# Step sizes of a selective-scan layer: projected on four column groups of the array and expanded in a series by another engine

## The chip, the core and the metric

The kernel runs on one core of a Trainium2 chip. The metric is the device time of one execution in microseconds, taken as the median of several runs. In what follows PE is the matrix engine (PEld its weight loads), DVE the vector engine, ACT the scalar engine, POOL the GpSimd engine and SP the engine that issues most transfers; SBUF is the on-chip memory, PSUM the memory that PE writes to, in banks of 128 x 512 floats.

## What is computed

The input is 4 sequences of 1,024 tokens with 256 features, in float32. A mixer layer comes first, then a mixture of experts; each is added to its input and normalised. What matters here is how the mixer gets its step sizes:

```python
zxbcdt = u @ in_proj_w.T                       # 512 z, 768 xBC, 8 dt columns
A  = -jnp.exp(A_log).mean(axis=0)              # 8 heads
z, xBC, dt = jnp.split(zxbcdt, [512, 1280], axis=-1)
xBC = silu(causal_conv_of_4(xBC) + conv_b)
x, Bm, Cm = jnp.split(xBC, [512, 640], axis=-1)
dt = softplus(dt + dt_bias)                    # one step per token and head
dA = exp(dt * A)
h  = h * dA + x * (dt * Bm)                    # for each token in turn
y  = h @ Cm + D * x
y  = rmsnorm(y) * silu(z);  x1 = layernorm(u + y @ out_proj_w.T)
```

After that x1 goes through a shared expert and through the two of eight experts that a softmax router chooses, and through a second layer normalisation.

## The kernel before, in words

The 4,096 tokens are worked in 8 tiles of 512 and 32 chunks of 128 (four chunks to a tile). For each tile, `turn_u` transposes the input into `uT`, `channels` projects and convolves the six groups of 128 xBC channels, and `steps` makes the step sizes of the tile, 128 tokens x 32 numbers (four chunks, eight heads). For each chunk the recurrence is worked as matrix products: `decays` loads running decays from DRAM and scans them on DVE, `turn_x` transposes x, B and C, `within` and `across` form the output and pass the state `h` on, `mix_out` gates and projects, `deviations` normalises, `turn_x1` transposes the result and `shared` runs the shared expert. `route` and `scatter` choose experts and scatter the rows to DRAM by indirect transfers that POOL issues. After the chunks, 71 blocks of 128 rows go through their experts (`chosen`), and `finish` normalises and writes out.

`steps` is a chain of six pieces. `project` (L435) multiplies the tokens, as 128 x 128 weights, with 8 columns of the projection matrix `win`, for four chunks and two halves of the features: 8 matmuls in source, 16 passes in the trace, since each float32 matmul is two. `begin` (L448) adds the bias on DVE and forms w = -|x|. `exponential` (L460) takes exp(w) on ACT. `series`, `series_on` and `step` (L463 to L489) work softplus on DVE as max(x, 0) + 2 atanh(w / (w + 2)), with a polynomial of five coefficients in q = s*s, and end with `dt` and `a` = dt * A. `step_decays` (L494) then sums `a` along the tokens on PE (a transpose, L502, and three products, L504), takes exponentials on ACT, and sends the decays to DRAM, from where `decays` loads them.

The order of work is written out by hand: `put(place, f)` gives each piece a place in time, the pieces are sorted by place and issued in that order, so that every engine has a fixed queue. A chunk has a slot of 16.4 places. The steps of tile n+2 stand in the fourth slot of tile n (L1514), those of tiles 0 and 1 at the start (L1488, L1503); `step_decays` of a tile stands in the first slot of the tile before it. PSUM has three banks `ps_m` for chunk work, two `ps_h` for expert products, two `ps_p` for projections (with `uT` transposes and the steps), one `ps_z`.

The piece `one` of `turn_x1` (L867) writes a row of ones over row 0 of the transposed x1, by POOL, once a chunk; the shared expert's first products then carry the biases in that row.

The loads of `win` are cut in pieces (L166 to L172): on SP its last 8 columns, then xBC columns 256 to 511, then 512 to 767, then z; on ACT xBC columns 0 to 255.

Of the kernel before, what the change touches and what calls it, by code (L numbers as in the profile page):

```python
# [8 lines left out]
F32 = mybir.dt.float32  # L9
# [3 lines left out]
ALU = mybir.AluOpType  # L13
# [15 lines left out]
D_PROJ = D_INNER + CONV_DIM + N_HEADS  # L29
# [4 lines left out]
NSUB = T // P  # L34
# [13 lines left out]
SERIES = (0.33333334, 0.19999853, 0.14296179, 0.10853288, 0.11612165)  # L48
# [9 lines left out]
R_DTB = 0  # L58
R_ALOG = R_DTB + N_HEADS
# [6 lines left out]
def kernel(  # L66
# [17 lines left out]
    nc = tc.nc  # L84
# [25 lines left out]
    ps_p = pool_in(ctx, "ps_p", 2, space=PSUM)  # L110
# [12 lines left out]
    def bc(ap, shape):  # L123
        return ap.to_broadcast(shape)
# [7 lines left out]
    def put(place, f, *args):  # L132
        pieces.append((place, len(pieces), f, args))
# [23 lines left out]
    win = const.tile([P, KD, D_PROJ], F32, name="win")  # L157
    rows_sb = const.tile([P, R_ALL], F32, name="rows_sb")
# [54 lines left out]
    a_neg = const.tile([P, N_HEADS], F32, name="a_neg")  # L213
# [182 lines left out]
    def by_head(t):  # L396
        return t.rearrange("p (c h) -> p c h", h=N_HEADS)

    def head_row(ap):
        return bc(ap.unsqueeze(1), [P, NSUB, N_HEADS])  # L400

    def bank(pool, tag, name):
        return pool.tile([P, T], F32, tag=tag, name=name)
# [21 lines left out]
        put(s + places[1], out_of, 0)  # L425
        put(s + places[2], out_of, 1)

    def steps(at, s, places=(0.0, 1.9, 3.2, 6.8, 10.8, 13.0), ps=(ps_p, "pp")):

        st = tile_state[at]  # L430

        def small(tag, n=NS):
            return k2.tile([P, n], F32, tag=tag, name=f"{tag}_{at}")

        def project():  # L435
            uT = st["uT"]
            pd = st["pd"] = bank(*ps, f"pd_{at}")
            for c in range(NSUB):
                for k in range(KD):
                    nc.tensor.matmul(  # L440
                        pd[:, c * N_HEADS : (c + 1) * N_HEADS],
                        uT[:, k, c * P : (c + 1) * P],
                        win[:, k, D_PROJ - N_HEADS :],
                        start=(k == 0),
                        stop=(k == KD - 1),
                    )

        def begin():  # L448
            x = st["dt_x"] = small("dt_x")
            nc.vector.tensor_tensor(  # L450
                by_head(x), by_head(st["pd"][:, :NS]), head_row(rows_sb[:, R_DTB:R_ALOG]),
                ALU.add,
            )

            w = st["dt_w"] = small("dt_w")
            nc.vector.scalar_tensor_tensor(w, x, -1.0, x, ALU.mult, ALU.min)

        def exponential():  # L460
            nc.scalar.activation(st["dt_w"], st["dt_w"], AF.Exp)

        def series():  # L463
            w = st["dt_w"]
            s = small("dt_s")
            nc.vector.tensor_scalar_add(s, w, 2.0)
            nc.vector.reciprocal(s, s)
            nc.vector.tensor_mul(s, s, w)
            q = small("dt_q")
            nc.vector.tensor_mul(q, s, s)  # L470
            acc = small("dt_acc")
            nc.vector.tensor_scalar_mul(acc, q, SERIES[4])
            st.update(dt_s=s, dt_q=q, dt_acc=acc)

        def series_on():
            q, acc = st["dt_q"], st["dt_acc"]
            for x in SERIES[3:0:-1]:
                nc.vector.scalar_tensor_tensor(acc, acc, x, q, ALU.add, ALU.mult)

        def step():  # L480
            q, acc, s, x = st["dt_q"], st["dt_acc"], st["dt_s"], st["dt_x"]
            nc.vector.scalar_tensor_tensor(acc, acc, SERIES[0], q, ALU.add, ALU.mult)
            nc.vector.scalar_tensor_tensor(acc, acc, 1.0, s, ALU.add, ALU.mult)
            nc.vector.tensor_scalar_max(x, x, 0.0)
            dt = small("dt")
            nc.vector.scalar_tensor_tensor(dt, acc, 2.0, x, ALU.mult, ALU.add)
            a = small("a")
            nc.vector.tensor_tensor(by_head(a), by_head(dt), head_row(a_neg), ALU.mult)
            st.update(dt=dt, a=a)  # L489

        for place, f in zip(places, (project, begin, exponential, series, series_on, step)):
            put(s + place, f)

    def step_decays(at, s, places=(0.0, 3.3, 7.5), ps=(ps_p, "pp")):  # L494
# [358 lines left out]
    def turn_x1(k):  # L853
        ch = chunk_state[k]

        def turn():
            pt = ch["ptx"] = bank(ps_m, "ps", f"ptx_{k}")
            for j in range(KD):
                nc.tensor.transpose(
                    pt[:, j * P : (j + 1) * P], ch["x1"][:, j * P : (j + 1) * P], ident  # L860
                )

        def copy():
            x1T = ch["x1T"] = k3.tile([P, KD, P], F32, tag="x1T", name=f"x1T_{k}")
            nc.scalar.copy(x1T.rearrange("p k t -> p (k t)"), ch["ptx"][:, :D])

        def one():  # L867
            nc.gpsimd.memset(ch["x1T"][0:1, 0], 1.0)

        return {"ptx": turn, "x1T": copy, "one": one}  # L870

# [596 lines left out]
    for k in range(NCHUNK + 1):  # L1468
        ps = deviations(k)
# [15 lines left out]
    H2 = (ps_h, "ph")  # L1485
    turn_u(0, -25.0)
    channels(0, 0, -20.9, -11.0)
    steps(0, -19.2, (0.0, 1.9, 2.4, 2.7, 2.7, 2.7), H2)  # L1488
    for c, s in zip(range(1, NCC), (-17.4, -15.7, -14.0, -10.0, -8.3)):
        channels(0, c, s, max(s + 5.0, -10.9), H2 if c in (2, 4) else (ps_p, "pp"))  # L1490
    step_decays(0, -12.4, (0.0, 0.9, 6.0), H2)
# [8 lines left out]
    load_shared(2.0)  # L1500
    for j in range(3):
        put((2 + j) * SLOT, clear_sum, j)
    steps(1, -0.3, (0.0, 8.0, 9.0, 15.5, 18.5, 21.5))  # L1503
    n_first = 0
    for k in range(NCHUNK):
        at, i = divmod(k, NSUB)
        s = k * SLOT
# [120 lines left out]
```

## Time and profile before

| | |
|---|---|
| median of 3 runs | 881.39 us (879.44 to 884.99) |
| profiled execution: its own time | 876.08 us |
| its span, first to last instruction | 874.1 us |
| around the span | 2.0 us |
| granted PE clock, mean | 0.983 |
| PE busy | 821.5 us (94%) |
| DVE busy | 588.2 us (67%) |
| ACT busy | 449.8 us (51%) |
| POOL busy | 425.2 us (49%) |

The busy shares are means over two stages: the chunks, up to about 575 us, and the blocks that overlap with their end and run on to the end. Times on a line of the timeline are the start from the beginning of the span, then how long the instructions of that line took together, engine, source line, operation, tiles, count, and in brackets how long the engine had been idle before and what released it.

### The profile page before, as it was taken

Reading aid. Unit: us, or ns where it says so; the run is one execution under the profiler, and the core shown is the slowest. Engines: PE = TensorE matmul, PEld = TensorE weight load, DVE = VectorE, ACT = ScalarE, POOL = GpSimd, SP = SyncE. Lnnn points to the kernel's source line nnn. Section 1 sums busy time; section 2 is a strip of 40 time slices with the busy share of each in tenths; the row PEclk is TensorE's granted clock in tenths of the full one; section 3 lists DMA queues with packets and bytes.
Section 4 is the critical chain, followed back from the end, with each engine's and each line's share of the span. In section 5 each row is a group of like instructions: output and inputs, shape, how many; then the busy total and the mean of one; then the engine's idle time right before and its main releaser. Section 6 shows DMA issues by size and latency. Waiting matters only on the chain.

```text
span 874.1 us, 13379 instructions
## 1 busy us (share of the span) xinstructions
PE 821.5 (94%) x3795; PEld 574.0 (66%) x3795; DVE 588.2 (67%) x1549; ACT 449.8 (51%) x1069; POOL 425.2 (49%) x563
## 2 busy tenths in 40 slices
PE   7789999999999999999998999899999999999980
PEld 4556677766767767666655776677677777776660
DVE  5897878878878879798788666245833333366653
ACT  4465657556657466676464455354444444444430
POOL 3253434457556556456724843624733333365443
PEclk9899999999999999999999999999999999999996
DMA  5547263174274363343321631335644432467764
GB/s 152 164 96 252 59 158 91 38 166 91 82 170 93 99 143 90 112 122 93 106 76 44 188 73 25 86 74 117 147 63 66 62 56 31 85 165 169 170 158 113
DMA packets 89381, 94.92 MB, mean 109 GB/s; under 512 B 15831, under 2 KB 78813, under 8 KB 89309
## 3 DMA queue, kind: packets, MB, share of 16 engines
q1 hardware_dynamic: 68030, 67.08, 26.3%
q0 software_dynamic: 18464, 24.33, 17.9%
q10 hardware_dynamic: 2816, 2.67, 1.0%
q8 instruction: 32, 0.52, 0.3%
q14 instruction: 39, 0.32, 0.1%
HBM read 61.22 MB, written 32.83 MB: 108 GB/s over the span
## 4 chain that ended last, share of the span: by engine, by line
PE 55%; issue 13%; DVE 11%; POOL 10%; DMA 7%; ACT 3%; POOLq 0%; SPq 0%; DVEq 0%; ACTq 0%
PE ph_s L883 6%; PE pp L554 6%; PE ph_c L883 6%; PE py L730 6%; POOL acc L1363 6%; PE pmo L815 5%; PE pz L632 5%; PE po_s L917 5%; DMA acc<-yb_c,to_c 4%; DVE xbc L572 3%; DMA fin<-acc 3%; PE po_c L917 3%; PE pi L751 2%; PE pst L767 2%; POOL xs L1102 2%
## 5 line engine op out<-in xcount | busy, mean ns | idle before, releaser
L883 PE MATMUL ph_c<-w,xgT_c 128*128 x568 | 193.0, 463 | 4.9 <-DVE xgT_c L1336 3.6
L1363 POOL DMA_INDIRECT acc<-yb_c,to_c x71 | 114.6, 1614 | 156.8 <-ACT yb_c L1357 95.5
L883 PEld LDWEIGHTS ph_c<-w,xgT_c 128*128 128x128 f32 x568 | 97.1, 190 | 47.9 <-DVE xgT_c L1336 5.6
L895 DVE TENSOR_TENSOR hid<-h_c,ph_c 128x352 f32<-128x352 f32 x71 | 36.9, 519 | 126.1 <-PE ph_c L883 118.5
L572 DVE SCALAR_TENSOR_TENSOR xbc<-pp,cols_sb,xbc 128x509 f32<-128x509 f32 x144 | 107.1, 745 | 16.3 <-ACT tail L580 8.9
L917 PE MATMUL po_c<-w,hT_c 128*128 x426 | 104.3, 381 | 1.2 <-ACT hT_c L912 1.2
L901 ACT ACTIVATE hid<-hid 128x352 f32<-128x352 f32 x103 | 51.8, 502 | 87.9 <-DVE hid L895 81.2
L554 PE MATMUL pp<-uT,win 128*128 128x512 f32 x192 | 92.0, 605 | 0.6 <-ACT dec L511 0.5
L883 PE MATMUL ph_s<-sw,x1T 128*128 128x352 f32 (+1 forms) x256 | 82.9, 465 | 2.1 <-issue 1.4
L763 POOL TENSOR_TENSOR y<-y,yi 128x512 f32<-128x512 f32 x28 | 35.5, 1267 | 99.5 <-ACT yi L757 79.7
L1102 POOL DMA_INDIRECT xs<-x,r_idx x64 | 73.4, 1147 | 20.5 <-issue 11.5
L917 PEld LDWEIGHTS po_c<-w,hT_c 128*128 128x128 f32 x426 | 75.5, 190 | 9.5 <-ACT hT_c L912 1.7
L657 DVE TENSOR_TENSOR_SCAN el<-da,ident 128x512 f32<-128x512 f32 x64 | 78.4, 1227 | 0.0
L883 PEld LDWEIGHTS ph_s<-sw,x1T 128*128 128x128 f32 x256 | 48.0, 191 | 35.1 <-issue 13.2
L890 ACT COPY h_c<-ph_c 128x352 f32<-128x352 f32 x71 | 32.1, 453 | 62.8 <-PE ph_c L883 54.4
L730 PEld LDWEIGHTS py<-xdt,el 128*128 128x128 f32 x512 | 62.4, 193 | 1.4
L815 PE MATMUL pmo<-wout,yT 128*128 128x256 f32 x256 | 61.4, 383 | 0.3 <-ACT yT L810 0.2
L730 PE MATMUL py<-xdt,el 128*128 128x64 f32 x512 | 61.3, 273 | 0.0
L632 PE MATMUL pz<-win,uT 128*128 128x512 f32 x128 | 61.2, 601 | 0.0
L587 ACT ACTIVATE xbc<-xbc 128x512 f32<-128x512 f32 x48 | 30.1, 629 | 58.7 <-DVE xbc L582 39.0
L757 ACT ACTIVATE yi<-pi,dec 128x64 f32<-128x64 f32 x224 | 49.0, 330 | 13.2 <-PE pi L751 10.6
L563 ACT ACTIVATE xbc<-pp,cols_sb 128x512 f32<-128x512 f32 x48 | 37.3, 779 | 34.9 <-PE pp L554 32.4
(214 smaller groups left out, 1548.4 us busy)
## 6 DMA issues: line engine op xcount, KB each, us to landing
da<-dad SPq DMA_DIRECT2D x64, 256.0 KB
xg_c<-xs SPq DMA_DIRECT2D x71, 130.0 KB
fin<-acc SPq DMA_DIRECT2D x32, 256.0 KB
w<-in_w_dram SPq DMA_DIRECT2D x16, 352.0 KB
w<-neg_d POOLq DMA_DIRECT2D x16, 352.0 KB
acc<-pad SPq DMA_DIRECT2D x3, 1408.0 KB
x<-in_u_dram SPq DMA_DIRECT2D x32, 128.0 KB
acc<-acc SPq DMA_DIRECT2D x32, 128.0 KB
```

Of the source, the lines that this page charges most:

```text
L554: nc.tensor.matmul(pp, win[:, k, D_INNER + c * P : D_INNER + (c + 1) * P], st["uT"][:, k], start=(k == 0), stop=(k == KD - 1),)
L572: nc.vector.scalar_tensor_tensor(cv[:, o:], hold["pp"][:, : T - o], cols_sb[:, cw + j : cw + j + 1], cv[:, o:], ALU.mult, ALU.add,)
L632: nc.tensor.matmul(pz, st["uT"][:, j, tok], win[:, j, :D_INNER], start=(j == 0), stop=(j == KD - 1),)
L657: nc.vector.tensor_tensor_scan(el, ch[f"da{j}"], ident4.rearrange("p h t -> p (h t)"), 0.0, ALU.mult, ALU.add)
L730: nc.tensor.matmul(py[:, hd], m, ch["xdt"][:, hd], start=True, stop=True)
L757: nc.scalar.activation(yi[:, hd], ch["pi"][:, hd], AF.Copy, scale=st["dec"][:, h0 + h : h0 + h + 1],)
L815: nc.tensor.matmul(po[:, :D], ch["yT"][:, c * P : (c + 1) * P], wout[:, c], start=(c == 0), stop=(c == NYC - 1),)
L883: nc.tensor.matmul(pw[:, : rhs.shape[-1]], hold["xT"][:, k], rhs, start=(k == 0), stop=(k == KD - 1),)
L901: nc.scalar.activation(t[:, :H], t[:, :H], AF.Silu)
L917: nc.tensor.matmul(po[:, :D], hold["hT"][:, c * P : (c + 1) * P], weights(None, c), start=(c == 0), stop=(c == HCK - 1),)
L1102: s = nc.gpsimd.indirect_dma_start(out=xs, out_offset=bass.IndirectOffsetOnAxis(ap=idx[:, j : j + 1], axis=0), in_=x1, in_offset=None, bou ...
L1363: s = nc.gpsimd.indirect_dma_start(out=accd[b % 2], out_offset=bass.IndirectOffsetOnAxis(ap=hold["to"], axis=0), in_=hold["yb"], in_offset ...
```

## The change

The eight matmuls of `project` swap their operands. The projection columns become the weights (the last 32 columns of `win`: 24 xBC columns and the 8 of dt) and the tokens stream through, 128 at a time; the four chunks go to four groups of 32 array columns and so to four groups of 32 partitions of a PSUM bank, chunk by chunk within each half of the features. Two pieces are added behind it: `copy`, in which ACT copies the 128 x 128 result to SBUF, and `turn`, a transpose on PE into a second bank. `begin` reads the 8 useful columns of each 32. In the series DVE keeps w + 2 (now halved, so that the factor 2 at the end goes away) and the reciprocal; the rest is 14 small POOL instructions, with the polynomial in two halves, in place of 11 DVE instructions. The places of the pieces change with it. `one` becomes a copy of a row of ones by ACT.

```diff
-    def steps(at, s, places=(0.0, 1.9, 3.2, 6.8, 10.8, 13.0), ps=(ps_p, "pp")):
+    def steps(at, s, places=(0.0, 0.6, 1.6, 2.0, 3.2, 6.8, 10.8, 13.0), ps=(ps_p, "pp")):
...
         def project():
             uT = st["uT"]
-            pd = st["pd"] = bank(*ps, f"pd_{at}")
-            for c in range(NSUB):
-                for k in range(KD):
+            pd = st["pdT"] = bank(*ps, f"pdT_{at}")
+            for k in range(KD):
+                for c in range(NSUB):
                     nc.tensor.matmul(
-                        pd[:, c * N_HEADS : (c + 1) * N_HEADS],
+                        pd[32 * c : 32 * c + 32, :P],
+                        win[:, k, D_PROJ - 32 :],
                         uT[:, k, c * P : (c + 1) * P],
-                        win[:, k, D_PROJ - N_HEADS :],
                         start=(k == 0),
                         stop=(k == KD - 1),
+                        tile_position=(0, 32 * c),
                     )
+        def copy():
+            st["dtT"] = k1.tile([P, P], F32, tag="dtT", name=f"dtT_{at}")
+            nc.scalar.copy(st["dtT"], st["pdT"][:, :P])
+        def turn():
+            pd = st["pd"] = bank(*ps, f"pd_{at}")
+            nc.tensor.transpose(pd[:, :P], st["dtT"], ident)
...
         def series():
             w = st["dt_w"]
-            s = small("dt_s")
-            nc.vector.tensor_scalar_add(s, w, 2.0)
+            s, q, q2, lo, hi = (small(f"dt_{n}") for n in ("s", "q", "q2", "lo", "hi"))
+            nc.vector.tensor_scalar(s, w, 2.0, 0.5, ALU.add, ALU.mult)
             nc.vector.reciprocal(s, s)
-            nc.vector.tensor_mul(s, s, w)
-            q = small("dt_q")
-            nc.vector.tensor_mul(q, s, s)
-            acc = small("dt_acc")
-            nc.vector.tensor_scalar_mul(acc, q, SERIES[4])
+            pool.tensor_tensor(s, s, w, ALU.mult)
+            pool.tensor_tensor(q, s, s, ALU.mult)
+            pool.tensor_tensor(q2, q, q, ALU.mult)
+            pool.tensor_scalar(hi, q, c4, c3, ALU.mult, ALU.add)
         def series_on():
-            for x in SERIES[3:0:-1]:
-                nc.vector.scalar_tensor_tensor(acc, acc, x, q, ALU.add, ALU.mult)
+            pool.tensor_scalar(lo, q, c2, c1, ALU.mult, ALU.add)
+            pool.tensor_tensor(hi, hi, q2, ALU.mult)
+            pool.tensor_tensor(hi, hi, lo, ALU.add)
+            pool.tensor_tensor(hi, hi, q2, ALU.mult)
+            pool.tensor_scalar(lo, q, c0, 1.0, ALU.mult, ALU.add)
         def step():
-            nc.vector.scalar_tensor_tensor(acc, acc, SERIES[0], q, ALU.add, ALU.mult)
-            nc.vector.scalar_tensor_tensor(acc, acc, 1.0, s, ALU.add, ALU.mult)
-            nc.vector.tensor_scalar_max(x, x, 0.0)
-            nc.vector.scalar_tensor_tensor(dt, acc, 2.0, x, ALU.mult, ALU.add)
-            nc.vector.tensor_tensor(by_head(a), by_head(dt), head_row(a_neg), ALU.mult)
+            pool.tensor_tensor(hi, hi, lo, ALU.add)
+            pool.tensor_tensor(hi, hi, s, ALU.mult)
+            pool.tensor_scalar(x, x, 0.0, None, ALU.max)
+            pool.tensor_tensor(dt, hi, x, ALU.add)
+            pool.tensor_tensor(by_head(a), by_head(dt), head_row(a_neg), ALU.mult)
...
         def one():
-            nc.gpsimd.memset(ch["x1T"][0:1, 0], 1.0)
+            nc.scalar.copy(ch["x1T"][0:1, 0], ones[0:1])
...
-    steps(0, -19.2, (0.0, 1.9, 2.4, 2.7, 2.7, 2.7), H2)
+    steps(0, -19.2, (0.0, 0.5, 0.9, 1.3, 1.8, 2.3, 2.3, 2.3), H2)
...
-    steps(1, -0.3, (0.0, 8.0, 9.0, 15.5, 18.5, 21.5))
+    steps(1, -0.3, (0.0, 4.0, 6.0, 8.0, 9.0, 14.5, 17.5, 20.5))
```

More of the change, by code (lines that the diff above doesn't have):

```diff
@@ L450, in begin @@
             nc.vector.tensor_tensor(
-                by_head(x), by_head(st["pd"][:, :NS]), head_row(rows_sb[:, R_DTB:R_ALOG]),
+                by_head(x), st["pd"][:, :P].rearrange("p (c h) -> p c h", c=NSUB)[:, :, 32 - N_HEADS :], head_row(rows_sb[:, R_DTB:R_ALOG]),
                 ALU.add,
@@ L461, in exponential @@
             nc.scalar.activation(st["dt_w"], st["dt_w"], AF.Exp)
+        c0, c1, c2, c3, c4 = (x * 0.25 ** (i + 1) for i, x in enumerate(SERIES))
+        pool = nc.gpsimd
         def series():
             w = st["dt_w"]
-            s = small("dt_s")
-            nc.vector.tensor_scalar_add(s, w, 2.0)
+            s, q, q2, lo, hi = (small(f"dt_{n}") for n in ("s", "q", "q2", "lo", "hi"))
+            nc.vector.tensor_scalar(s, w, 2.0, 0.5, ALU.add, ALU.mult)
             nc.vector.reciprocal(s, s)
-            nc.vector.tensor_mul(s, s, w)
@@ L469, in series @@
-            q = small("dt_q")
-            nc.vector.tensor_mul(q, s, s)
-            acc = small("dt_acc")
-            nc.vector.tensor_scalar_mul(acc, q, SERIES[4])
-            st.update(dt_s=s, dt_q=q, dt_acc=acc)
-        def series_on():
-            q, acc = st["dt_q"], st["dt_acc"]
-            for x in SERIES[3:0:-1]:
-                nc.vector.scalar_tensor_tensor(acc, acc, x, q, ALU.add, ALU.mult)
+            pool.tensor_tensor(s, s, w, ALU.mult)
+            pool.tensor_tensor(q, s, s, ALU.mult)
@@ new lines, in series @@
+            pool.tensor_tensor(q2, q, q, ALU.mult)
+            pool.tensor_scalar(hi, q, c4, c3, ALU.mult, ALU.add)
+            st.update(dt_s=s, dt_q=q, dt_q2=q2, dt_lo=lo, dt_hi=hi)
+        def series_on():
+            q, q2, lo, hi = (st[f"dt_{n}"] for n in ("q", "q2", "lo", "hi"))
+            pool.tensor_scalar(lo, q, c2, c1, ALU.mult, ALU.add)
[3 more added lines that the diff above has]
+            pool.tensor_scalar(lo, q, c0, 1.0, ALU.mult, ALU.add)
@@ L480, in step @@
         def step():
-            q, acc, s, x = st["dt_q"], st["dt_acc"], st["dt_s"], st["dt_x"]
-            nc.vector.scalar_tensor_tensor(acc, acc, SERIES[0], q, ALU.add, ALU.mult)
-            nc.vector.scalar_tensor_tensor(acc, acc, 1.0, s, ALU.add, ALU.mult)
-            nc.vector.tensor_scalar_max(x, x, 0.0)
+            lo, hi, s, x = (st[f"dt_{n}"] for n in ("lo", "hi", "s", "x"))
+            pool.tensor_tensor(hi, hi, lo, ALU.add)
+            pool.tensor_tensor(hi, hi, s, ALU.mult)
@@ L485, in step @@
+            pool.tensor_scalar(x, x, 0.0, None, ALU.max)
             dt = small("dt")
-            nc.vector.scalar_tensor_tensor(dt, acc, 2.0, x, ALU.mult, ALU.add)
+            pool.tensor_tensor(dt, hi, x, ALU.add)
             a = small("a")
-            nc.vector.tensor_tensor(by_head(a), by_head(dt), head_row(a_neg), ALU.mult)
+            pool.tensor_tensor(by_head(a), by_head(dt), head_row(a_neg), ALU.mult)
             st.update(dt=dt, a=a)
-        for place, f in zip(places, (project, begin, exponential, series, series_on, step)):
+        for place, f in zip(
+            places, (project, copy, turn, begin, exponential, series, series_on, step)
+        ):
```

## The prediction

> **What bounds the kernel now.** I read the sums by stage first, then the costs of the groups, then the order of PE around the steps, and last the places where PE waits. The first view gives busy time by stretches of 62.8 us, about four chunks (PE, PEld, DVE, ACT, POOL, then the granted clock):
>
> ```profile
> 83.80:146.60 62.80, 61.98 (x295) 42.92 (x295) 47.81 (x92) 39.98 (x99) 25.21 (x34) 1.00 0.45 114
> 335.00:397.80 62.80, 61.80 (x292) 42.48 (x292) 54.41 (x129) 40.42 (x104) 34.61 (x50) 1.00 0.42 108
> 397.80:460.60 62.80, 58.30 (x281) 40.60 (x281) 50.46 (x107) 35.62 (x81) 34.89 (x52) 0.97 0.35 96
> ```
>
> From 84 to 398 us PE is busy for 98 to 99%, so there a microsecond off PE is a microsecond off the time, and relief of DVE is worth nothing by itself. Before 84 us (55.0 of 62.8 us busy) and after 398 us PE waits for others. The groups that are touched, and the rows that price what is new:
>
> ```profile
> L440 PEld LDWEIGHTS pd<-win,uT 128*128 128x128 f32 x128 | 15.6, 192 | 4.0 <-issue 3.1 <-ACT uT L422 0.7 <-DMA neg<-in_w_dram 0.2
> L440 PE MATMUL pd<-win,uT 128*128 128x8 f32 x128 | 14.8, 251 | 0.0
> L689 ACT COPY b<-pb 128x128 f32<-128x128 f32 x32 | 8.2, 255 | 1.8 <-PE pb L682 1.8
> L502 PEld LDWEIGHTS pc<-ident,a 128*32 128x32 f32 x8 | 0.8, 96 | 4.6 <-DVE xbc L572 3.0 <-issue 1.0 <-ACT xbc L587 0.5
> ```
>
> The first two overlap, so what a tile pays is read from starts in the timeline:
>
> ```profile
> 83.00 1.85 PE L440 MATMUL pd<-win,uT 128*128 128x8 f32 x16
> 84.70 2.64 PE L883 MATMUL ph_s<-sw,x1T 128*128 128x352 f32 x8
> ...
> 103.43 1.88 PE L554 MATMUL pp<-uT,win 128*128 128x512 f32 x4
> 105.15 0.27 PE L502 MATMUL pc<-ident,a 128*32 128x128 f32 x1
> 105.15 0.30 PEld L504 LDWEIGHTS pc<-a,le 128*128 128x128 f32 x2 [0.33 <-issue]
> 105.26 0.31 PE L504 MATMUL pc<-a,le 128*128 128x32 f32 x2
> ```
>
> The old projection holds PE from 83.00 to 84.70: 1.70 us for 16 passes, 0.106 each, the spacing of 128-column weight loads. L502 is the one instruction that already uses 32 columns (128*32): its 128 streamed columns occupy PE for 0.11 us, and it starts when the product before it has streamed (103.43 + 4 x 0.43 = 105.15).
>
> POOL's price for small dependent instructions, its free time in a steps slot, and the one place where POOL sets the pace (the last four lines, from the chain of waits):
>
> ```profile
> 421.34 0.21 POOL L531 TENSOR_TENSOR part<-tail,cols_sb 128x12 f32<-128x12 f32 x1
> 421.63 0.21 POOL L536 TENSOR_TENSOR corr<-corr,part 128x12 f32<-128x12 f32 x1
> 421.92 0.21 POOL L531 TENSOR_TENSOR part<-tail,cols_sb 128x6 f32<-128x6 f32 x1
> ...
> 224.52 0.20 POOL L868 MEMSET x1T<- 1x128 f32 x1 [3.02 <-ACT x1T L865]
> 228.95 1.26 POOL L763 TENSOR_TENSOR y<-y,yi 128x512 f32<-128x512 f32 x1 [4.23 <-ACT yi L757]
> ```
>
> ```profile
> 430.41 0.28 POOL shift L843
> 430.72 0.60 ACT x L847
> 433.02 0.37 ACT hT_s L912
> 433.44 1.56 PE po_s L917 x6
> ```
>
> **The projection.** Removed: 1.70 us of PE a tile. Added: 16 passes of 128 streamed columns. If the four groups run fully side by side, 4 x 0.107 = 0.43 us; if a weight load of 0.096 stands ahead of every pass, 16 x (0.096 + 0.107) = 3.25 us. L502's load did not stand alone: PE shows no gap ahead of 105.15, and L504's loads run under L502's own product. So loads stay hidden. The two passes of one float32 matmul go to the same 32 columns, so I let them follow each other, and let only the next chunk's pass overlap. That makes pairs: 8 x 0.107 = 0.86 us. The transpose adds 0.11 (L502's spacing). Gain: 1.70 - 0.86 - 0.11 = 0.73 us a tile, between 1.16 and -1.66. [...]
>
> **The added wait.** `turn` on PE waits for ACT's copy, 0.255 us by L689. From tile 2 on the first shared-expert product (1.2 us) stands between them on PE, and ACT has finished `yi` at 84.09 when the projection ends at about 83.9: the copy is done by 84.4, the transpose due at 85.1. Without that cover it would cost about 0.5 us. For tile 1 the cover is missing (below). The second bank is no wait: both buffers that it could take were emptied by the `uT` copies that the projection itself needs.
>
> **DVE's relief.** 11 instructions a tile, 2.27 us by their means (0.19 each, 0.30 and 0.27 the longest). From 84 to 398 us PE covers DVE, so 0.
>
> **POOL's load.** 14 instructions a tile. Dependent ones stand 0.29 apart (421.34, 421.63, 421.92), nine of the gaps are dependent; independent ones 0.13 to 0.20 (r_info, 406.02, 406.15, 406.28): 9 x 0.29 + 5 x 0.2 = 3.6, taken as 3.8 us. The longest such rows (1.05 and 1.20 us) bound it at some 15 us, the shortest (0.13) at 1.8. They stand behind xw in POOL's queue, in tiles 4 to 7 partly ahead of the scatters. What covers them is POOL's idle time before y_yi or fade: 9.2 us in tile 2, 8.5 in tile 3, 7.3 in tile 4 (the two lines), 6.5 and 7.2 in tiles 5 and 6. So 0 there. In tile 7 POOL has no gap from 409.9 to 430.7: six scatter transfers, corr, four more, fade, roots, then ACT's normalisation waits for shift, hT_s stands behind that on ACT, and PE's po_s behind hT_s. There the 3.8 us go straight into the chain, less 0.2 for the memset: +3.6, less PE's 0.73: +2.9.
>
> **The ones.** 32 POOL memsets of 0.20 become ACT copies of 0.15 to 0.26 (L580, L689): 5 to 8 us of ACT, whose next work after x1T waits over 1 us for PE (97.40 to 98.75), while the shared product starts at 100.27. Cost 0. The only PE wait for a memset (0.9 us, before 422.60) lies ahead of the hT_s wait of tile 7, which takes it over: 0.
>
> **The start.** Tile 0's projection now also needs the load of xBC columns 512 to 767. Loads issued up to it are 1,356 KB; the transfer rates of the first 40 us add up to 1,389 KB at 7 us, and the projection starts at 9.1: no stall, at most 8.7 us (pp_4 reads them at 17.84 without a wait). POOL brings `a` about 1.2 us later than DVE did (15.93), PE's pc and pp_4 move by as much, and ACT's four silu then end near 22.6 instead of 23.3: a gain of up to 0.6. SP's decay store goes 1.2 us later; the decays had landed by 23 and are read at 28.55. Tile 1: ACT's copy stands behind silu of its first group, which waits for DVE:
>
> ```profile
> 39.87 0.63 ACT L587 ACTIVATE xbc<-xbc 128x512 f32<-128x512 f32 x1 [6.04 <-DVE xbc L582]
> ```
>
> The copy ends at 40.8 instead of leaving PE free to begin pb at 38.74, so pb, px and the next projection go 2.2 us later, of which 0.6 was idle anyway; DVE and ACT lose about 1.1. Then DVE, busy without a break from 43 to 57, drops 2.8 us of instructions (48.92 to 55.18). POOL's y_yi goes from 53.18 to about 55.3, which takes back 1 us. POOL's third weight correction is put behind four series pieces, about 3 us later, and is read at 68. Together -1.0, between -3.1 (all relief, no wait) and +2.2 (the wait, no relief).
>
> **Sum.** -1.0 for the start, 5 x -0.73 = -3.65 for tiles 2 to 6, +2.9 for tile 7: -1.75, so 876.08 becomes 874.3. The profiled execution lies 5.3 us below the median of the runs; on the median's scale 881.39 becomes **879.6 us**.
>
> **Rivals.**
> - Other side: POOL becomes late in every slot. DVE and POOL lengthen each other: corr took 1.05 us at 420.32, DVE's dt_w averages 0.75 with 0.19 at best. Against it, medians of 0.21 to 0.24. It decides from 0.5 us an instruction (7 us against gaps of 6.5 to 9.2). At 0.65 (9.1 us) tiles 3 to 6 lose 0.6, 1.8, 2.6 and 1.9, tile 7 8.2: -4.65 + 6.9 + 8.2 = +10.4, 891.8; at 0.75 about +19.
> - The groups don't overlap at all, loads hidden: 1.71 us, 0.12 lost a tile: -1.0 + 0.6 + 3.7 = +3.3, 884.7. With loads exposed: +8.3 (tiles 2 to 6) + 5.3 - 1.0 = +12.6, 894.0.
> - Faster: four groups side by side (5 x 1.16), all 3.1 us at the start, and tile 7's lateness given back later by idle PE: -8.9, 872.5.
>
> **How the numbers follow.** Forecast 0.60; no overlap 0.12; loads exposed 0.06; POOL late 0.12; all gains 0.10. A measurement of this kernel tells about 1% (8.8 us) from no change. Faster by over 1% is the last case, 0.10; within 1% the first two, 0.72; slower the loads and POOL, 0.18. Range 870 to 893: from the fast case, less the runs' scatter, to POOL at 0.65 us, leaving out exposed loads and POOL's worst.
>
> **What would show it.** Right: from the projection's first start to the next product 0.8 to 1.0 us, the transpose 0.11 without a wait from tile 2 on, y_yi still released by ACT's yi, a PE wait of about 4 us for hT_s near 433, pb of chunk 1 near 41. Wrong: a spacing of 0.2 per pass, POOL instructions over 0.5, y_yi released by series pieces, or a tile 0 projection that waits for its load.

## The result and the profile after

The changed kernel takes 882.59 us (median of 20 runs, 878.63 to 888.32), the kernel before, beside it on the same chip, 879.38 us (20 runs, 876.59 to 884.99). The ratio is 1.0032, 95% interval 1.0019 to 1.0045: slower by 0.3%, where 0.2% faster was forecast. The time lies in the forecast range. In the profiled executions the spans are 882.0 and 874.1 us.

To find the place, I compare when PE starts the four transposes `pt` of the gated product, once a chunk. A shift is that start less the start in the profile before. These sums of shifts by stage are worked out from the timelines, for the changed kernel and for the kernels of the experiments below ("in slots" are the four stretches between chunks 6-7, 10-11, 14-15 and 18-19, in which the steps of tiles 3 to 6 are projected; us, negative is earlier than before):

| kernel | start, to chunk 2 | tile 2 (2-3) | tiles 3-6, in slots | rest of 3-22 | tile 7's projection (22-23) | 23 to 25 | 25 to 31 |
|---|---|---|---|---|---|---|---|
| changed | -0.01 | -0.90 | +0.33 | -0.13 | -0.93 | **+7.64** | -0.27 |
| series on DVE | +0.76 | -0.90 | +0.36 | -0.13 | -0.94 | -0.71 | -0.23 |
| before, series on POOL | -3.38 | 0.01 | +0.13 | +4.26 | -0.01 | +6.02 | -0.40 |
| tile 7's series on DVE | -0.45 | -0.90 | +0.37 | -0.12 | -0.94 | +0.70 | -0.18 |
| projection only | +0.71 | -0.90 | +0.31 | -0.13 | -1.02 | -0.69 | -0.06 |
| norm behind hT_s | -1.92 | -0.90 | +0.35 | -0.14 | -0.93 | +0.77 | -0.07 |
| PE kept busy | -1.55 | -0.91 | +0.35 | -0.12 | -0.94 | +5.47 | -0.68 |
| begin late | -3.48 | -0.90 | -1.37 | +7.07 | +0.03 | +8.36 | -0.04 |
| copy early | -3.55 | -0.90 | +0.32 | -0.15 | -0.93 | +6.90 | -0.24 |
| second choice late | -2.81 | -0.90 | -3.14 | -0.21 | -0.51 | +6.90 | +2.25 |
| before, second choice late | +3.08 | 0.00 | -0.05 | +1.84 | +0.43 | 0.00 | +3.05 |
| ones by POOL | -1.43 | -0.90 | +0.32 | +2.40 | -1.02 | +6.40 | -0.27 |
| before, norm behind hT_s | +2.24 | 0.01 | +0.12 | -0.04 | -0.01 | -1.69 | -0.59 |
| all moves | -3.29 | -0.90 | -3.15 | -0.22 | -0.43 | -2.90 | +2.07 |
| all, second choice in the early tiles | -2.85 | -0.90 | -3.16 | -0.18 | -0.93 | -2.86 | -0.88 |
| the same, copy late | -3.68 | -0.90 | -3.15 | -0.18 | -0.93 | -2.86 | -0.11 |
| the same, tile 7's series on POOL | -3.67 | -0.90 | -3.16 | -0.18 | -0.93 | +0.73 | +0.88 |

Line numbers in what follows are those of each kernel itself. The middle columns repeat within 0.1 us from profile to profile, where the queues are the same. Two parts do not: the start (0 to +3.1 for three kernels whose start is that of before), and what the blocks add behind chunk 31 (-2.7 to +3.3 in all profiles, +2.2 in this one, in a stage that the change leaves alone). So a single pair of spans says little, and a stage of the table much.

The lines that answer to the old projection's 1.70 us. After, on PE, tile 2:

```profile
83.08 0.64 PE L442 MATMUL pdT<-uT,win 128*32 128x128 f32 x16
83.66 1.45 PE L902 MATMUL ph_s<-sw,x1T 128*128 128x352 f32 x4
84.94 0.27 PE L457 MATMUL pd<-ident,dtT 128*128 128x128 f32 x1
85.05 1.38 PE L902 MATMUL ph_s<-sw,x1T 128*128 128x360 f32 x4
```

The 16 passes hold PE from 83.08 to 83.66, 0.58 us, and the transpose for 0.11 us without a wait: 1.0 us less a tile, better than forecast. The table shows 0.90 and 0.93 of it kept in tiles 2 and 7, and nothing in tiles 3 to 6. Tile 4's slot, PE and then DVE (the bracket is the idle time ahead, and what ended it):

```profile
206.75 0.39 PE L878 MATMUL ptx<-ident,x 128*128 128x128 f32 x2
...
209.66 0.64 PE L442 MATMUL pdT<-uT,win 128*32 128x128 f32 x16
...
213.18 0.60 PE L704 MATMUL px<-ident,xbc 128*128 128x128 f32 x4
215.53 0.63 PE L823 MATMUL pt<-ident,xw 128*128 128x128 f32 x4 [1.75 <-DVE xw L805]
```

```profile
207.03 0.69 DVE L752 TENSOR_TENSOR y<-y,py 128x512 f32<-128x512 f32 x1 [0.60 <-PE py L749]
...
211.84 0.19 DVE L461 TENSOR_TENSOR dt_x<-pd,rows_sb 128x32 f32<-128x32 f32 x1 [0.53 <-PE pd L457]
212.06 0.99 DVE L469 SCALAR_TENSOR_TENSOR dt_w<-dt_x 128x32 f32<-128x32 f32 x1
...
214.71 0.68 DVE L805 TENSOR_TENSOR xw<-y,pz 128x512 f32<-128x512 f32 x1
```

From the end of PE's `py` DVE needs 8.4 us to the end of `xw` (207.03 to 215.39; before 8.2), idle only for the 0.53 us in which `dt_x` waits for the turn. PE's own work in that stretch is now 7.0 us, so it waits 1.75 us (before 0.68). Whatever PE saves there is returned as a longer wait. The same place in the profile before:

```profile
215.06 0.52 DVE L895 TENSOR_TENSOR hid<-h_s,ph_s 128x352 f32<-128x352 f32 x1 [0.23 <-ACT xdt L779]
215.58 0.68 DVE L786 TENSOR_TENSOR xw<-y,pz 128x512 f32<-128x512 f32 x1
216.40 0.63 PE L804 MATMUL pt<-ident,xw 128*128 128x128 f32 x4 [0.68 <-ACT x L692]
```

DVE's only slack on this way was the 0.23 us that it stood idle ahead of `hid` (tile 6 the same, tiles 3 and 5 none). The bracket of `pt` names ACT's copy x, but `pt` starts 0.15 us after the end of `xw` in each of these slots, before and after. Tile 7's place before (POOL, then PE) and after (PE, ACT and POOL):

```profile
409.65 0.26 POOL L843 TENSOR_SCALAR shift<-stat 128x1 f32<-128x1 f32 x1
...
430.41 0.27 POOL L843 TENSOR_SCALAR shift<-stat 128x1 f32<-128x1 f32 x1
...
433.44 1.56 PE L917 MATMUL po_s<-sw_sb,hT_s 128*128 128x256 f32 x6 [0.75 <-ACT hT_s L912]
434.84 1.89 PE L730 MATMUL py<-xdt,el 128*128 128x64 f32 x16
```

```profile
425.46 0.28 PE L521 MATMUL pc<-ident,a 128*32 128x128 f32 x1 [2.06 <-POOL a L505]
...
437.23 2.93 PE L936 MATMUL po_s<-sw_sb,hT_s 128*128 128x256 f32 x6 [6.30 <-ACT hT_s L931]
439.95 2.78 PE L749 MATMUL py<-xdt,el 128*128 128x64 f32 x16
```

```profile
434.51 0.60 ACT L866 ACTIVATE x<-x,shift,stat 128x256 f32<-128x256 f32 x1 [6.48 <-POOL shift L862]
435.13 1.28 ACT L527 ACT_TABLE_LOAD   x1
...
436.72 0.46 ACT L931 COPY hT_s<-pt_s 128x384 f32<-128x384 f32 x1
```

```profile
407.90 0.26 POOL L862 TENSOR_SCALAR shift<-stat 128x1 f32<-128x1 f32 x1
...
410.13 1.16 POOL L483 TENSOR_TENSOR dt_s<-dt_s,dt_w 128x32 f32<-128x32 f32 x1
...
421.24 0.21 POOL L491 TENSOR_SCALAR dt_lo<-dt_q 128x32 f32<-128x32 f32 x1
...
425.16 0.25 POOL L505 TENSOR_TENSOR a<-dt,a_neg 128x32 f32<-128x32 f32 x1
...
432.20 1.10 POOL L383 TENSOR_SCALAR stat<-stat 128x2 f32<-128x2 f32 x1
...
434.21 0.27 POOL L862 TENSOR_SCALAR shift<-stat 128x1 f32<-128x1 f32 x1
```

POOL has no gap from 408 to 437, but for some 0.3 us ahead of each scatter transfer. The three pieces of the series hold it from 410.13 to 412.25, 421.24 to 422.67 and 423.89 to 425.35, 5.0 us together; `shift` ends up 5.55 us later behind the previous chunk's `shift` than before (26.31 us against 20.76). ACT's normalisation waits for it, `hT_s` stands behind that on ACT, PE's `po_s` behind `hT_s`. PE waits 6.30 us (before 0.75: 5.55 us more), and then `po_s` and `py` take 2.93 and 2.78 us where 1.56 and 1.89 were seen before: another 2.2 us. The granted clock is 0.50 in the first of the two.

### The profile page after: what moved, and what is told of

It is laid out like the page before. It is cut to its first block, busy times and chain, and to the rows that moved or that the text cites. A ratio compares the mean times of both kernels' runs of the same rounds, so it can differ in the third digit from the quotient of the medians.

```text
span 882.0 us, 13404 instructions
## 1 busy us (share of the span) xinstructions
PE 818.9 (93%) x3803; PEld 564.8 (64%) x3803; DVE 570.7 (65%) x1461; ACT 458.7 (52%) x1109; POOL 453.6 (51%) x643
## 4 chain that ended last, share of the span: by engine, by line
PE 53%; issue 14%; POOL 10%; DVE 10%; DMA 9%; ACT 3%; SPq 1%; POOLq 0%; DVEq 0%; ACTq 0%
PE pp L573 7%; PE ph_s L902 6%; PE py L749 6%; POOL acc L1382 6%; PE pmo L834 6%; PE pz L651 5%; DMA acc<-yb_c,to_c 5%; PE po_s L936 5%; PE ph_c L902 5%; DMA fin<-acc 3%; PE pi L770 2%; DVE xbc L591 2%; PE po_c L936 2%; PE pst L786 2%; POOL xs L1121 2%
## 5 line engine op out<-in xcount | busy, mean ns | idle before, releaser
L573 PE MATMUL pp<-uT,win 128*128 128x512 f32 x192 | 95.4, 624 | 1.7 <-ACT uT L422 1.2
L936 PE MATMUL po_s<-sw_sb,hT_s 128*128 128x256 f32 x192 | 48.3, 389 | 7.2 <-ACT hT_s L931 7.2
```

The costliest lines, as they stand in the source:

```text
L573: nc.tensor.matmul(pp, win[:, k, D_INNER + c * P : D_INNER + (c + 1) * P], st["uT"][:, k], start=(k == 0), stop=(k == KD - 1),)
L936: nc.tensor.matmul(po[:, :D], hold["hT"][:, c * P : (c + 1) * P], weights(None, c), start=(c == 0), stop=(c == HCK - 1),)
```

## The experiments

Each is an edit of the changed kernel unless it says "before". Ratios are to the kernel before, with 95% intervals.

### Which part costs: the series, and where

**Series on DVE.** All of the series as in the kernel before, the rest as changed.

```diff
-            pool.tensor_tensor(s, s, w, ALU.mult)
...
+            nc.vector.tensor_mul(s, s, w)
...
```

> The changed kernel with the whole series back on DVE (the 11 instructions of before); the projection on four column groups, its copy and turn, and the ones by ACT stay. Theory (POOL's queue at tile 7 makes the loss): the 7.8 us that the changed kernel loses between chunks 24 and 25 are gone, PE's wait for hT_s near 433 is under 1.5 us and po_s takes about 1.6 us again; but the start keeps its wait for the copy without DVE's relief behind it, so the gated transposes of chunk 2 start 1.5 to 3 us later than before, and tiles 3 to 6 keep nothing of the cheaper projection. End of the span -1 to +2 us against before, ratio 0.998 to 1.003. Rival (the projection's own steps cost the time: the wait of DVE for the turn, the transposes, the copies on ACT): the transposes of chunk 25 still start at 449 or later, ratio 1.004 or more.

874.75 us, ratio 0.9948 (0.9925 to 0.997), better than either theory had it. Chunks 23 to 25 cost 0.7 us less than before instead of 7.6 more. PE still waited 2.73 us for `hT_s` there, not under 1.5 as expected, but `po_s` took 1.56 us; chunk 2 came 0.76 us later than before, not 1.5 to 3. The projection, its copy and turn are not what costs.

**Before, series on POOL.**

```diff
-            nc.vector.tensor_mul(s, s, w)
...
+            pool.tensor_tensor(s, s, w, ALU.mult)
...
```

> The kernel before with the series on POOL alone; projection, ones by POOL and all places of before. Theory: DVE's relief at the start makes chunk 2 about 1 us earlier, nothing is gained or lost in tiles 3 to 6, and between chunks 24 and 25 the queue of POOL costs 6 to 8 us as in the changed kernel, with an idle stretch of PE of over 5 us near 431 to 437 and po_s slowed to some 2.9 us behind it. End of the span +4 to +8 us, ratio 1.003 to 1.009. Rival (the projection's steps cost it): no loss at tile 7, ratio 1.000 or less.

884.9 us, 1.006 (1.0037 to 1.0084). The loss at tile 7 is there (+6.0), in another form: the memset stands behind the series in POOL's queue. The same cost a stretch that I had not expected, 3.6 us between chunks 15 and 16 (PE, then POOL):

```profile
289.69 4.35 PE L888 MATMUL ph_s<-sw,x1T 128*128 128x352 f32 x8 [2.05 <-POOL x1T L873]
```

```profile
289.25 0.25 POOL L493 TENSOR_TENSOR a<-dt,a_neg 128x32 f32<-128x32 f32 x1
289.45 0.19 POOL L873 MEMSET x1T<- 1x128 f32 x1
```

At the start, with DVE's relief alone, chunk 2 comes 3.4 us earlier in this one profile than in the profile before.

**Tile 7's series on DVE**, the other tiles' on POOL.

```diff
+        if at == NTILE - 1:
+            def series():
+                w = st["dt_w"]
...
+        else:
```

> The changed kernel with the series of the last tile alone worked by DVE, as before. Theory: the start's relief and tile 7's projection are kept, the queue of POOL among the scatters is as before: the gated transposes of chunk 25 start at 443 to 444 (changed kernel 451.1, before 445.1), PE waits under 1.5 us for hT_s there and po_s takes about 1.6 us; ratio to before 0.996 to 0.999. Rival (POOL's instructions cost a little in every slot, and tile 7 is only where it shows): a lateness of 3 us or more remains at chunk 25, ratio 1.002 or more.

872.06 us, 0.991 (0.9882 to 0.9937): 7 us below the kernel before, and 10 below the changed kernel, for one tile's 14 instructions. The table shows 6.9 of these 10 between chunks 23 and 25; the rest is not assigned (the profiled execution, 875.67 us, was the slowest of six). PE still waited 2.49 us there, not under 1.5 as expected, and ran slowly behind it:

```profile
430.44 2.51 PE L968 MATMUL po_s<-sw_sb,hT_s 128*128 128x256 f32 x6 [2.49 <-ACT hT_s L963]
```

The rival, a small cost of POOL in every slot, is out: the middle columns are those of the changed kernel.

**Projection only**: series on DVE, ones by POOL.

```diff
-            nc.scalar.copy(ch["x1T"][0:1, 0], ones[0:1])
+            nc.gpsimd.memset(ch["x1T"][0:1, 0], 1.0)
```

> The changed kernel with the series on DVE and the ones by POOL: of the change only the projection, its copy and its turn are left. Theory: within 1 us of the kernel with ACT's ones (the ones cost and bring nothing but the 0.7 to 0.9 us wait of PE near 422 ahead of the shared product), so end of the span -1 to +2.5 us against before, ratio 0.998 to 1.004. Rival (ACT's 32 copies delay what stands behind them): over 2 us faster than the kernel with ACT's ones.

876.78 us, 0.9974 (0.9953 to 0.9994). The stages agree with those of "series on DVE"; the 2.0 us between the two medians lie within the intervals.

### How POOL's lateness reaches PE at tile 7

**Norm behind hT_s** in ACT's queue.

```diff
-        "roots": (0, 8.9), "norm": (0, 13.2),
+        "roots": (0, 8.9), "norm": (0, 14.4),
```

> The changed kernel with one piece moved: ACT's normalisation stands behind the copy hT_s instead of ahead of it, in every chunk; POOL's queue stays as it is. Theory (the loss at tile 7 reaches PE only because hT_s stands on ACT behind a normalisation that waits for POOL's shift): PE's wait of 6.3 us for hT_s near 431 to 437 and the slow po_s and py behind it are gone, though POOL's shift comes as late as before (434 to 436 less the lead); the gated transposes of chunk 25 start at 442.5 to 445, ratio to before 0.994 to 0.999. What stays is PE's 2.1 us wait for POOL's a near 425. Rival (POOL's lateness reaches PE by other ways too: the decays, the sum with yi, the transposes of the normalised x1): PE waits 3 us or more at another place within the next two chunks, ratio 1.001 or more.

873.12 us, 0.9943 (0.9923 to 0.9963). Chunks 23 to 25 lose 0.8 instead of 7.6 us, with POOL's queue as late as before:

```profile
423.58 0.28 PE L521 MATMUL pc<-ident,a 128*32 128x128 f32 x1 [2.08 <-POOL a L505]
...
428.88 1.46 PE L936 MATMUL po_s<-sw_sb,hT_s 128*128 128x256 f32 x6
430.18 1.89 PE L749 MATMUL py<-xdt,el 128*128 128x64 f32 x16
433.30 0.44 PE L878 MATMUL ptx<-ident,x 128*128 128x128 f32 x2 [1.23 <-ACT x L866]
```

The wait for `hT_s` and the slow products are gone, the waits for `a` and for the normalised x1 are left. So ACT's order carried the lateness.

**PE kept busy** with products that nobody reads; they add work and leave none out.

```diff
+    def warm():
+        junk = bank(*H2, "junk")
+        for _ in range(6):
+            nc.tensor.matmul(junk, ident, win[:, 0, :T], start=True, stop=True)
+    put(24 * SLOT + 15.0, warm)
```

> The changed kernel with six products that nobody reads (512 columns, float32, two passes each, 5.2 us of PE) put into PE's queue in the idle stretch of tile 7, between the projection of the mixer's output and po_s. Theory (PE's clock is lowered by the 6.3 us of idleness and this costs 2.2 us on top of the wait): po_s takes about 1.6 us instead of 2.93 and py 1.9 instead of 2.78, chunk 25 starts about 2.2 us earlier than in the changed kernel (1.3 to 2.5), ratio to before 1.000 to 1.002. Rival (po_s and py are slow because of what runs beside them, the weight correction's transfer or POOL): po_s stays at 2.5 us or more and nothing is gained.

From chunk 24 to 25 it takes 22.43 instead of 24.61 us: the 2.2 us of the theory, with the wait for `hT_s` still ending the stretch and the granted clock at 1.00 behind it:

```profile
435.74 1.56 PE L936 MATMUL po_s<-sw_sb,hT_s 128*128 128x256 f32 x6 [1.18 <-ACT hT_s L931]
437.14 1.90 PE L749 MATMUL py<-xdt,el 128*128 128x64 f32 x16
```

The median, 875.96 us, 0.9969 (0.9951 to 0.9988), is lower than expected by more than these 2.2 us explain; the rest of it stays open.

**Ones by POOL**, the series on POOL as changed.

```diff
-            nc.scalar.copy(ch["x1T"][0:1, 0], ones[0:1])
+            nc.gpsimd.memset(ch["x1T"][0:1, 0], 1.0)
```

> The changed kernel with the ones by POOL's memset again, the series on POOL as changed. Theory (the kernel with the series alone lost 3.6 us between chunks 15 and 16 because the memset stood behind the series and the scatters in POOL's queue and PE's shared product waited 2.05 us for it and then ran at a lower clock): the same here, a wait of PE for the memset in one or more of the slots behind chunks 7 to 23 and 2 to 4 us lost in each, ratio 1.004 to 1.010. Rival (the ones are worth nothing, as the forecast had it): within 1 us of the changed kernel up to chunk 22.

880.89 us, 1.0034 (1.0015 to 1.0053). One slot, not several, lost 1.9 us (chunks 15 to 16, a wait of 2.00 us for the memset), and at tile 7 the memset took over the wait for `hT_s`:

```profile
426.64 5.12 PE L902 MATMUL ph_s<-sw,x1T 128*128 128x352 f32 x8 [7.08 <-POOL x1T L887]
```

The ratio is just below my bound: one slot instead of several lost time, at full speed behind the wait (`ph_s` in 2.66 us, 2.56 without a wait), and at tile 7 the memset's wait stands in the place of the one for `hT_s` and costs 1.2 us less (6.40 against 7.64).

### Why tiles 3 to 6 keep nothing

**Begin late**: `begin` and the exponential behind `xw`.

```diff
-places=(0.0, 0.6, 1.6, 2.0, 3.2, 6.8, 10.8, 13.0)
+places=(0.0, 0.6, 1.6, 4.2, 4.6, 6.8, 10.8, 13.0)
```

> The changed kernel with the piece begin (dt_x and dt_w on DVE) and the exponential put behind the gated product xw and the first of the products with the decays, in tiles 2 to 7. Theory (the cheaper projection is worth nothing in tiles 3 to 6 because DVE's queue, in which begin now waits for the turn, ends later than PE there): PE's wait of 1.75 us ahead of the gated transposes of those slots falls under 0.8, each of tiles 3 to 6 keeps 0.9 us or more, chunk 20 starts at 355.5 to 357.5 (changed kernel 360.1, before 360.8). Behind it tile 7 loses what it did; end of the span 3 to 6 us below that of the changed kernel, ratio 0.997 to 1.001. Rival (the lost time goes to another place: the exponential now stands ahead of the shared expert's silu on ACT and makes PE wait for pt_s): nothing is kept, chunk 20 at 360 or later.

886.37 us, 1.0096 (1.0071 to 1.0121): the rival. In tile 4's slot

```profile
213.49 0.63 PE L823 MATMUL pt<-ident,xw 128*128 128x128 f32 x4 [1.20 <-DVE xw L805]
213.96 1.88 PE L651 MATMUL pz<-win,uT 128*128 128x512 f32 x4
217.23 0.55 PE L925 MATMUL pt_s<-ident,hid 128*128 128x128 f32 x3 [1.39 <-ACT hid L920]
```

the first wait shrinks by 0.55 us only and another takes its place: the exponential, now late, stands ahead of the shared expert's silu on ACT. The slots keep 1.4 us, the chunks between them lose 7.1, and chunk 20 starts at 362.2, later than in either kernel.

**Second choice late**: six other DVE instructions taken out of the same stretch.

```diff
-((s + 7.3, s + 11.7, s + 16.9) if soon else (s + 3.9, s + 6.7, s + 14.9))
+((s + 7.3, s + 15.2, s + 16.9) if soon else (s + 3.9, s + 10.2, s + 14.9))
```

> The changed kernel with the router's second choice (six small DVE instructions, 1.3 us) put behind the gated product xw and the products with the decays. The run with begin moved showed that its own form of the theory fails, so a new form is tested: in the slots of tiles 3 to 6 the way from PE's py over DVE's queue (8.4 us from y_py to xw) is as long as PE's own work between py and pt, so a shorter projection only lengthens PE's wait ahead of pt. Theory: with 1.3 us off DVE's queue there, PE's wait of 1.75 us falls to about 0.8 us (the rest is ACT's copy x, which frees the bank), each of tiles 3 to 6 keeps 0.8 to 1.0 us, and the shift of chunk 20 against that of chunk 4 in the same run grows by 3 to 4 us. Ratio to before 0.996 to 1.001. Rival (something else than DVE's queue holds PE there): the wait stays above 1.4 us and the shift of chunk 20 is that of chunk 4 within 1 us.

Tiles 3 to 6 now keep 0.68, 0.89, 0.66 and 0.91 us, 3.1 together; the wait in tile 4's slot is down to 0.68 us:

```profile
210.99 0.63 PE L823 MATMUL pt<-ident,xw 128*128 128x128 f32 x4 [0.68 <-DVE xw L805]
```

DVE's queue it was. What remains is not a wait for ACT's copy x, as I had expected: x ended 0.12 us after this `pt` had started. The median, 879.99 us (1.0029, 1.0008 to 1.005), misses the expected ratio: tile 7 costs 6.9 us as before, and the move loses 2.3 us behind chunk 25, where I had applied it to the later tiles too.

**Before, second choice late**, the same edit.

> The kernel before with the same move of the second choice. Theory: there the wait ahead of pt is 0.68 us and is ended by ACT's copy x, so that DVE's shorter queue brings nothing: chunk 20 against chunk 4 within 1 us of before, ratio 0.998 to 1.002; the gain of the moved choice in the changed kernel is then that of its cheaper projection. Rival (the move is worth as much without the projection): 2.5 us or more earlier at chunk 20, ratio 0.997 or less.

In the four slots the shift is -0.05 us in all: without the cheaper projection the move gains nothing there, as the theory has it. Its reason, ACT's copy x, does not hold; what the lines of tile 4 show is that PE's wait of 0.68 us stays although DVE now stands idle for 1.96 us ahead of `hid`, until ACT's `xdt`:

```profile
218.68 0.52 DVE L895 TENSOR_TENSOR hid<-h_s,ph_s 128x352 f32<-128x352 f32 x1 [1.96 <-ACT xdt L779]
...
220.02 0.63 PE L804 MATMUL pt<-ident,xw 128*128 128x128 f32 x4 [0.68 <-ACT x L692]
```

So 0.68 us is what is left of the wait when DVE's queue is not late. Elsewhere the move costs (1.1 us between chunks 15 and 16, 3 us behind chunk 25), so 883.74 us, 1.0062 (1.0038 to 1.0087), outside my range.

### The start

**Copy early**: ACT's copy of tile 1 ahead of the silu.

```diff
-    steps(1, -0.3, (0.0, 4.0, 6.0, 8.0, 9.0, 14.5, 17.5, 20.5))
+    steps(1, -0.3, (0.0, 3.2, 6.0, 8.0, 9.0, 14.5, 17.5, 20.5))
```

> The changed kernel with tile 1's copy on ACT put ahead of the silu that waits for DVE. Theory (the start loses 3.1 us at chunk 0 by the turn's wait for that copy and the slow products behind it, while DVE's relief is worth 3.4 us there, as the kernel with the series alone shows): the turn of tile 1 no longer waits, chunk 0 starts 1 to 2 us earlier than before instead of 3.1 later, chunk 2 2.5 to 4 us earlier than before instead of 0, and this is kept to chunk 24. Tile 7's loss stays, so the end comes 2.5 to 4 us ahead of the changed kernel, ratio to before 0.998 to 1.001. Rival (chunk 2 is set by something else than PE's order at the start, which is why the 3.1 us were made up): chunk 2 within 1 us of the changed kernel.

878.65 us, 1.0008 (0.9991 to 1.0025); chunk 2 is 3.55 us earlier than before. But "begin late", with the same start as the changed kernel, reached -3.48 with the wait for the copy in place. What differs most is the clock. The stretches 32-38 and 38-44 us of the changed kernel and of "begin late" (the third number from the right is the granted clock):

```profile
32.00:38.00 6.00, 4.79 (x35) 3.01 (x34) 5.44 (x9) 0.83 (x2) 3.64 (x7) 0.80 0.97 302
38.00:44.00 6.00, 4.24 (x12) 2.78 (x12) 4.36 (x10) 3.56 (x8) 2.88 (x5) 0.50 0.71 210
```

```profile
32.00:38.00 6.00, 3.35 (x34) 2.24 (x22) 5.84 (x9) 0.59 (x1) 3.26 (x7) 1.00 1.00 302
38.00:44.00 6.00, 4.76 (x20) 2.85 (x21) 4.42 (x10) 5.44 (x11) 3.79 (x5) 1.00 0.61 189
```

Of eight profiles with this start five had a lowered clock there (the projection `pp` behind the turn took 2.55 to 3.62 us, in the other three 1.88); of four with the early copy none (1.88). That the wait makes it likelier fits, and is not settled by so few. Nor is the clock all that moves the start: "before, second choice late" has the latest of all (+3.08) at a granted clock of 1.00 from 26 to 50 us.

### The parts together

**All moves**: tile 7's series on DVE, norm behind `hT_s`, copy early, second choice late, by the edits above.

> The changed kernel with all that the runs point to: the last tile's series on DVE, the normalisation behind hT_s on ACT, tile 1's copy ahead of the silu, the second choice behind xw. If the parts add up: 872.1 us of the kernel with the last tile's series on DVE, less some 3 us of the copy, 3.6 us of the second choice and 2 to 3.5 us of the wait for hT_s that was left there: 862 to 866, ratio 0.980 to 0.986. Rival (the relieved stretches meet one common other bound, DVE or the loads of the decays): ratio 0.988 or more.

866.33 us, 0.9874 (0.9849 to 0.99), just short of the sum; 2.1 us were lost behind chunk 25.

**All moves, second choice late in the early tiles only.**

```diff
-... if soon else (s + 3.9, s + 6.7, s + 14.9)
+... if soon else (s + 3.9, s + 10.2, s + 14.9)
```

> All moves of the kernel before this one, but the second choice moved only in the tiles up to the first cut, where the router's slot is the slot of the steps; in the later tiles it stays where it was. Theory: chunk 27 follows chunk 26 by 16.8 us again instead of 19.1, PE's wait for the sum x1 near 462 is about 0.6 us instead of 1.9; median 862.5 to 865.5, ratio 0.981 to 0.986. Rival (the 2.4 us have another cause): ratio as before, 0.987 or more.

**863.72 us, 0.9832 (0.9817 to 0.9848): faster than both kernels.** PE's wait for x1, first with the move in all tiles, then in the early ones:

```profile
461.76 0.66 PE L910 MATMUL ptx<-ident,x 128*128 128x128 f32 x2 [1.90 <-DVE x L877]
```

```profile
460.55 0.41 PE L910 MATMUL ptx<-ident,x 128*128 128x128 f32 x2 [0.65 <-DVE x L877]
```

**The same, copy late.** The copy's place back at 4.0.

> The same with tile 1's copy at the changed kernel's place, behind the silu. Theory (the turn's wait for the copy is time that PE had to spare at the start; what differs between profiles is the clock granted near 32 to 44 us): median within 1.5 us of the kernel with the early copy, ratio 0.981 to 0.988. Rival (the wait costs what the first profile showed): 2.5 us or more slower than with the early copy.

865.62 us, 0.9859 (0.9842 to 0.9876): 1.9 us slower, between the two expectations, with touching intervals. What the copy's place is worth stays open.

**The same, tile 7's series on POOL.** The branch for the last tile is left away.

> All moves, but the last tile's series on POOL as in the changed kernel. Theory: with the normalisation out of the way of hT_s, POOL's lateness at tile 7 reaches PE only by pc's wait for a (2.1 us) and the transposes of the normalised x1 (1.2 us): 2 to 3.5 us slower than with the series on DVE there, no slow po_s. Rival (once the order on ACT is mended POOL's queue costs nothing): within 1 us of the kernel with the series on DVE.

868.62 us, 0.9893 (0.9876 to 0.991): 4.9 us slower, more than either expectation. In the table 1.8 us of it lie behind chunk 25. From chunk 23 to 25 the difference is 3.6 us: 2.05 of waiting for `a`, and 1.6 in the next projection (3.44 us, 1.88 at full speed), which ran slowly behind that wait:

```profile
418.25 0.28 PE L521 MATMUL pc<-ident,a 128*32 128x128 f32 x1 [2.05 <-POOL a L505]
...
419.78 3.44 PE L651 MATMUL pz<-win,uT 128*128 128x512 f32 x4
```

**Before, norm behind hT_s**, the edit as above.

> The kernel before with the normalisation moved behind hT_s and nothing else. Theory: there POOL's shift comes early enough, PE waits only 0.75 us for hT_s at tile 7, so the move gains 0 to 1.5 us, ratio 0.998 to 1.000. Rival (the move is worth as much by itself, the gain has little to do with the change): 4 us or more, ratio 0.995 or less.

878.21 us, 0.9997 (0.9975 to 1.0019). Alone the move is worth nothing that can be measured; its gain is the removal of the change's own loss.

## Why the prediction was wrong

The forecast was 1.75 us faster, and the medians are 3.2 us apart the other way. Two steps failed: that PE covers DVE in tiles 2 to 6, so that each keeps what PE saves, and the size of tile 7's loss. The start erred the other way by some 2.7 us; that the time lies in the range is in part this luck.

- **The projection** was right in kind and too cautious: 0.58 us instead of 0.86, and the transpose 0.11 us without a wait. The passes did not overlap in pairs: in tile 2 they start in four sets of four, 0.007 us apart within a set, the sets 0.11 to 0.13 us apart. Their 16 loads took 0.38 us together, from 83.08 on, beside the passes; the 3.25 us that the prediction worked out for a load ahead of every pass were not seen.
- **"5 x -0.73 = -3.65 for tiles 2 to 6" failed** in four of the five. Tile 2 kept 0.90; tiles 3 to 6 gave +0.33 together. The step read "from 84 to 398 us PE covers DVE, so 0" from stage sums. In the slot in which the router's choices also stand, DVE's queue from `py` to `xw` is the longer way as soon as PE is faster. The profile before showed it, not by PE's wait of 0.68 us ahead of `pt`, which stays when DVE has time to spare, but by DVE's idle time ahead of `hid`: 0.23 us in tiles 4 and 6 and none in tiles 3 and 5, so that no more than that could be kept. The instructions taken off DVE stand behind `xw`, and `begin` ahead of it got a new wait. Taking 1.3 us off that stretch gave 3.1 us back; with the old projection it gave none.
- **"Tile 7: +2.9"** had the right chain and less than half of the size: -0.93 for its projection and +7.64 behind, 6.7 us. Two terms failed. The "+3.6" for POOL measured 5.55: its 14 instructions took 5.0 us, not 3.8 (0.9 of that is the first product, which ran beside a DVE scan, see the last section), and the rest of its queue about 0.5 us more. And the slower products behind the wait were put at nothing: 2.2 us, which the run with PE kept busy took away. Adding POOL's lateness to PE's lead was right: the lead reached POOL's queue too (`shift` of the chunk before stands at 407.90 instead of 409.65). The wait of 2.06 us for `a` took the place of what before lost there to the memset and a lowered clock (chunks 23 to 24: 18.21 against 18.35 us).
- **"The ones: cost 0"** holds for the cost. They were worth 1.9 us between chunks 15 and 16, since the memset would have come behind the series.
- **"The start: -1.0"** cannot be read from the one pair of profiles (-0.01). Over all of them, eight with this start lie at -1.9 in the mean (0.0 to -3.7) and three with the start of before at +1.8 (0 to +3.1), so about -3.7, an estimate from few and scattered profiles: the bound with all of the relief was the better value. `pb` of chunk 1 came at 40.41, near the 41 forecast.
- **The sum** with these terms, -3.7 - 0.9 + 0.3 - 0.1 - 0.9 + 7.6 - 0.3, is +2.0 us, against 3.2 between the medians and -1.75 on record. The other 1.2 us are not assigned; the part behind chunk 31 alone moves by more.
- **The rivals**: POOL late in every slot did not happen (0.21 to 0.25 us for most instructions, though over 1 us for the first product in tiles 2 to 7; `y` still released by ACT's `yi` or the DVE chain); no overlap and exposed loads are excluded by the 0.58 us.

## What to carry to other kernels

A stage in which an engine is 98% busy can still have one stretch a tile in which another engine's queue is the longer way, or becomes it as soon as the busy engine is faster: before counting a saving, see how long the other engine stands idle ahead of the place where the two meet, and ask whether the instructions that are taken away stand ahead of that place or behind it. Work moved to an engine that is idle on average is paid where its queue is full, and here it was the order of a third engine's queue that brought it to the critical one; there, moving one consumer behind its neighbour can be worth more than the change (0.77 us lost at tile 7 instead of 7.64). A wait can cost more than its length: here 2.2 us more, for two slower products behind it, the first at a granted clock of 0.50.

## What the hardware showed beyond that

- The slow products: after 6.30 us of idleness the six passes of `po_s` took 2.93 us, where 1.46 is usual without a wait, half the speed, at a granted clock of 0.50. In the chunks, the idle stretches of 4.65 to 7.08 us were all followed by it: `po_s` took 2.93 us behind 4.65, 4.71, 6.30 and 6.31 us, and `ph_s` 5.03 and 5.12 us, where 2.56 is usual, behind 7.07 and 7.08 us. Of the shorter ones, for example, 1.90 us (ahead of `ptx` in "all moves", with `pi` behind it in 2.05 instead of 1.02 us), 2.05 us (the memset in "before, series on POOL", then `ph_s` in 4.35 us, and `pc` in "the same, tile 7's series on POOL", then the projection in 3.44 instead of 1.88 us) and 2.49 us (tile 7's series on DVE, `po_s` in 2.51 us) were; 2.00 us in "ones by POOL" (`ph_s` in 2.66 us) and 2.06 us ahead of `pc` in the changed kernel (the projection in 1.88 us) were not, nor 2.73 us in the kernel with the series on DVE:

```profile
431.88 1.56 PE L934 MATMUL po_s<-sw_sb,hT_s 128*128 128x256 f32 x6 [2.73 <-ACT hT_s L929]
```

  So the length of a wait alone does not decide; what else does was not measured.
- Single instructions of POOL and of DVE took longer beside a 512-column instruction of the other. The first product of the series on POOL took 1.16 us at 410.13, where its successors took 0.21 to 0.30. In tiles 2 to 7 it took 1.04 to 1.17 us and ended 0.04 to 0.05 us after a 512-column DVE scan that had begun before it; in tiles 0 and 1, with no such scan beside it, it took 0.25 us. The other way round, DVE's `dt_w` took 0.99 us in tile 4 and ended 0.05 us after POOL's 512-column product of `h`, which had begun 0.09 us before it; alone it took 0.19 us in tile 0. What makes them longer was not measured.
